# Six-layer block with a state-space scan: the four sums over states of a group are tied to the last of their four operands

## The chip, the cores and the metric

One core of one Trainium2 chip runs the whole program. The metric is the time of one execution in microseconds on the device (us), lower is better; the time before is the median of three runs.

## The reference

The input is x of shape 4 x 512 x 128 (batch, position, feature). Six residual layers follow one another: a fast-feedforward "tree" attention, a 16-head attention, the tree attention again, a mixture of 8 experts and one shared expert, a Mamba block, and the mixture again. The change lies in the Mamba block. Cut to what matters:

```
x_dbl = x @ W_x;  dt = softplus(x_dbl[..., :64] @ W_dt + b_dt)
Bm = x_dbl[..., 64:80];  Cm = x_dbl[..., 80:96];  A = -exp(A_log)      # 256 channels, 16 states
def step(h, inp):                                                      # over 512 positions
    dA = exp(dt_t[..., None] * A)
    h  = dA * h + (dt_t * x_t)[..., None] * B_t[:, None, :]
    y  = einsum('bdn,bn->bd', h, C_t)                                  # sum over the 16 states
    return h, y
y = ys + x * D;  y = y * silu(z);  out = y @ W_out;  return residual + out
```

## The kernel before

**Tiling of the scan.** `state_main` handles one batch entry b. The 256 channels are two halves c; each half is four blocks g of 32 channels; the 16 states are four groups q of four states. One tile `states` has 128 partitions, which are 32 channels times four states, and 512 positions. So a batch entry needs 2 x 4 x 4 = 32 such tiles, the four of them 128. Each goes through four steps: ScalarE takes the exponential into `decay` (L970), VectorE multiplies B with dt*x into `states` (L971) and runs the recurrence over it in place (L972), GpSimd multiplies by C in place (L973). Here "the product" is L973.

**The sums.** For one (c, q), here a "group", the function `sums` gives TensorE four matmuls (L934). Each takes one of the four `states` tiles of the group as moving operand and the constant `gather` of 128 x 32 as weights, and writes 32 partitions of the bank `state_acc`: g = 0 to 3 write partitions 0-31, 32-63, 64-95 and 96-127. The operands are f32, and each such matmul appears in the trace as two instructions, so that a group is eight. The four groups q of a half accumulate in the same bank, then `close` (L943) takes it on VectorE. There are 32 groups, 128 sums, 256 instructions.

**The order of the work.** The layers of the four batch entries overlap. Each layer of each entry is a job with planned start and end (`TIMES`), and the program is written by stepping the job that is due first. Inside `state_main`, `Later` delays the call of `sums` by five steps (`LAG_STATE`), so that it is written behind the first step of the group after next. Then the framework's scheduler lays out the order of each engine: in a simulated time of its own, an engine takes, of the instructions that are ready, the one that was written first. An instruction that is not ready when the engine is free is therefore passed by later ones of other jobs. The order so found is fixed in the program, and on the chip every engine goes through its own list in order and waits on semaphores. The four matmuls of a group are written next to one another, but nothing keeps them together: each becomes ready with its own product.

**Buffers.** `states` has eight buffers, two groups' worth; a buffer is free when its sum has read it. `state_b` (the spread B of a group, L958) has two banks, `state_acc` one.

**What else runs beside the scan.** The mixture layers' matmuls: three for each product of split operands (L173 to L175, tile `moe`), then `moe_acc` (L773), with ScalarE's tanh (L758) and VectorE's products (L759, L765) between them; GpSimd adds their results to x (L784).

Of the kernel before, what the change touches and what calls it, by code (L numbers as in the profile page):

```python
# [112 lines left out]
def macaron(ctx: ExitStack, tc: tile.TileContext, t: dict, stages: int = 6):  # L113
    nc = tc.nc
# [6 lines left out]
    def bank(role):  # L121
        return psum.tile([P, S], F32, tag=role, name=role, bufs=BANKS[role])
# [19 lines left out]
    def work(role, shape=(S,), dtype=F32):  # L142

        return wp.tile([P, *shape], dtype, tag=role, name=role, bufs=BUFS[role])
# [11 lines left out]
    def flat(a):  # L156
        return a if len(a.shape) == 2 else a.rearrange("p a b -> p (a b)")
# [763 lines left out]
    def spread(out, rows):  # L921

        nc.sync.dma_start(out=out, in_=rows.unsqueeze(1).to_broadcast([CH, OF_GROUP, S]))

    def state_main(b, st, consts):
        A = consts()[0]
        xs, sz, cs = st.xs, st.sz, st.cs
        accs = {}

        def sums(c, q, hs):  # L930
            if q == 0:
                accs[c] = bank("state_acc")
            for g in range(4):
                nc.tensor.matmul(  # L934
                    accs[c][32 * g : 32 * g + 32, :],
                    lhsT=gather,
                    rhs=hs[g],
                    start=(q == 0),
                    stop=(q == GROUPS - 1),
                )  # L940

        def close(c):
            nc.vector.scalar_tensor_tensor(  # L943
                xs[:, c, :], xs[:, c, :], at["D"][:, c : c + 1], accs[c], ALU.mult, ALU.add
            )
            nc.gpsimd.tensor_mul(xs[:, c, :], xs[:, c, :], sz[:, c, :])

        later = Later(LAG_STATE)
        for c in range(2):
            dt, dtx = work("dts", (4, S)), work("dtxs", (4, S))  # L950
            rows = t["state_rows"][b, c].rearrange("m (g r) s -> m g r s", r=CH)
            for g in range(4):
                for m, to in enumerate((dt, dtx)):
                    spread(to[:, g, :], rows[m, g])
            for q in range(GROUPS):

                bs = bank("state_b")
                nc.tensor.matmul(  # L958
                    bs,
                    lhsT=spread_b[:, ts(q, P)],  # L960
                    rhs=st.xb,
                    start=True,
                    stop=True,
                )
                hs = []
                for g in range(4):
                    k = (4 * c + g) * GROUPS + q
                    dA, h = bank("decay"), work("states")
                    hs.append(h)
                    nc.scalar.activation(dA, dt[:, g, :], AF.Exp, scale=A[:, k : k + 1])  # L970
                    nc.vector.tensor_mul(h, bs, dtx[:, g, :])  # L971
                    nc.vector.tensor_tensor_scan(h, dA, h, 0.0, ALU.mult, ALU.add)  # L972
                    nc.gpsimd.tensor_mul(h, h, cs[:, q])  # L973
                    later.step()
                    yield
                later.add(partial(sums, c, q, hs))
                if q == GROUPS - 1:
                    later.add(partial(close, c))
        while later.queue:
            later.step()  # L980
            yield
        ps = bank("state_tr")
        for i in range(NT):
            for c in range(2):
                nc.tensor.matmul(
                    ps[:, ts(i, P)],
                    lhsT=xs[:, c, ts(i, P)],
                    rhs=w_out[:, c, :],
                    start=(c == 0),
                    stop=(c == 1),  # L990
                )
        nc.vector.tensor_add(flat(x[b]), flat(x[b]), ps)
# [12 lines left out]
    def once(f):  # L1005
        made = []

        def get():
            if not made:
                made.append(f())  # L1010
            return made[0]

        return get
# [5 lines left out]
    heads, states = once(head_consts), once(state_consts)  # L1019
# [46 lines left out]
    def add_state(name):  # L1066
        b, (p0, p1, m0, m1) = int(name[1]), TIMES[name]
        st = State()
        p = job(p0, p1, 13, state_prep(b, st, states), *needs(done[b]))
        done[b] = job(m0, m1, 33 + LAG_STATE, state_main(b, st, states), p)  # L1070
# [261 lines left out]
```

## Time and profile before

| | |
|---|---|
| median of 3 runs (lowest to highest) | 1149.53 us (1147.91 to 1149.95) |
| the profiled execution, its own time | 1150.85 us |
| its span, first to last instruction | 1149.1 us |
| TensorE busy | 1080.6 us (94%) |
| VectorE busy | 909.7 us (79%) |
| ScalarE, GpSimd busy | 517.1 us (45%), 411.6 us (36%) |

The names are PE for TensorE, PEld for its weight loads, DVE for VectorE, ACT for ScalarE, POOL for GpSimd. A busy PE includes the modelled ends of pipelined matmuls, which overlap the next ones, so the distance from one start to the next tells more than a duration. In rows of the timeline the columns are start, duration, engine, line, operation, output and inputs, shapes, count, and in brackets the idle time before and what ended it.

### The profile page before, as it was taken

To read this page: it belongs to the slowest core of one execution; us is meant where nothing else is said; L and a number is where in the kernel's file an instruction comes from. 1 tells how busy PE (TensorE), PEld (TensorE's weight loads), DVE (VectorE), ACT (ScalarE), POOL (GpSimd) and SP (SyncE) were. 2 spreads that over 40 slices of the span, in tenths; PEclk is the share of its full clock that TensorE was granted. 3 is DMA by queue.
4 is the path that set the end of the run, shared out by engine and by line. 5 is a ranking of instruction groups with operands and counts; after the bars stand their busy time and mean duration, and the time that the engine had idled before them with its cause. 6 is when DMAs were issued, how large, how long until landed. Compare 5 with 4: busy or idle time off the path is not lost.

```text
span 1149.1 us, 16519 instructions
## 1 busy us (share of the span) xinstructions
PE 1080.6 (94%) x5536; PEld 715.5 (62%) x5536; DVE 909.7 (79%) x2199; ACT 517.1 (45%) x1078; POOL 411.6 (36%) x396
## 2 busy tenths in 40 slices
PE   3999999999999999999999999998798989998998
PEld 2666566566665667765566676675276656655677
DVE  5566787577676677776789998799989999999864
ACT  2221423233332455544533643565476567454444
POOL 4115322002100141320314651266626656656623
PEclk9999999999999999999999999999899999999999
DMA  7787755231442122333752334662038323823310
GB/s 208 203 248 215 260 137 122 75 94 57 85 139 60 54 58 60 104 85 112 232 181 90 125 84 122 234 210 92 1 98 278 127 60 125 292 74 124 111 51 10
DMA packets 79653, 146.42 MB, mean 127 GB/s; under 512 B 7537, under 2 KB 39665, under 8 KB 79569
## 3 DMA queue, kind: packets, MB, share of 16 engines
q1 hardware_dynamic: 79280, 145.07, 42.1%
q8 instruction: 44, 0.72, 0.3%
q14 instruction: 41, 0.33, 0.1%
q10 hardware_dynamic: 288, 0.30, 0.1%
HBM read 125.35 MB, written 13.70 MB: 121 GB/s over the span
## 4 chain that ended last, share of the span: by engine, by line
PE 63%; DVE 20%; issue 6%; DMA 4%; POOL 3%; ACT 3%; SPq 1%; POOLq 0%; ACTq 0%; DVEq 0%
PE tree_acc L404 11%; PE moe_acc L773 7%; DVE states L972 6%; PE head_acc L601 5%; PE tree_mm L173 4%; PE head_max L557 4%; PE head_sc L633 3%; PE moe L173 3%; PE tree_mm L175 3%; PE tree_mm L174 3%; DVE states L971 3%; PE moe L174 3%; PE moe L175 3%; DVE u L759 2%; PE state_acc L934 2%
## 5 line engine op out<-in xcount | busy, mean ns | idle before, releaser
L973 POOL TENSOR_TENSOR states<-states,cs 128x512 f32<-128x512 f32 x128 | 163.4, 1282 | 161.9 <-DVE states L972 93.1
L404 PE MATMUL tree_acc<-full,ring 128*128 128x512 f32 x384 | 194.3, 598 | 5.2 <-DVE full L394 4.9
L565 DVE CUSTOM_DVE_ANT_0 head_max<-head_max,kept 128x128 f32<-128x128 f32 (+3 forms) x256 | 126.8, 496 | 64.1 <-PE head_max L557 61.9
L394 DVE SCALAR_TENSOR_TENSOR full<-tree_mm,kept,mask 128x512 f32<-128x512 f32 x188 | 138.5, 746 | 40.2 <-PE tree_mm L175 35.1
L649 ACT ACTIVATE pt<-head_sc 128x512 f32<-128x512 f32 (+1 forms) x176 | 95.0, 559 | 139.0 <-PE head_sc L641 138.3
L972 DVE TENSOR_TENSOR_SCAN states<-decay,states 128x512 f32<-128x512 f32 x128 | 154.6, 1216 | 0.5
L773 PEld LDWEIGHTS moe_acc<-ring,u 128*128 128x128 f32 x1152 | 141.4, 193 | 17.6 <-DVE u L765 3.0
L773 PE MATMUL moe_acc<-ring,u 128*128 128x128 f32 x1152 | 145.7, 278 | 1.0 <-DVE u L759 0.7
L173 PE MATMUL moe<-xl,ring 128*128 128x512 f32 x288 | 128.8, 448 | 8.9 <-DVE u L765 1.9
L784 POOL TENSOR_TENSOR kept<-kept,y 128x512 f32<-128x512 f32 x64 | 83.4, 1303 | 136.2 <-ACT y L783 118.8
L970 ACT ACTIVATE decay<-dts,kept 128x512 f32<-128x512 f32 x128 | 88.4, 693 | 88.1 <-DVE states L972 66.5
L758 ACT ACTIVATE u<-moe 128x512 f32<-128x512 f32 x144 | 86.3, 602 | 70.4 <-PE moe L175 66.5
L759 DVE SCALAR_TENSOR_TENSOR u<-u,moe 128x512 f32<-128x512 f32 x144 | 97.0, 677 | 23.4 <-ACT u L758 23.1
L174 PE MATMUL moe<-xh,ring 128*128 128x512 f32 x288 | 115.4, 401 | 0.0
L175 PE MATMUL moe<-xh,ring 128*128 128x512 f32 x288 | 115.0, 400 | 0.0
L541 POOL TENSOR_SCALAR km<-k_bias,kept 128x512 fp32r<-128x512 f32 x64 | 43.3, 697 | 171.3 <-PE head_sc L633 151.0
L783 ACT ACTIVATE y<-moe_acc,scratch 128x128 f32<-128x128 f32 x256 | 73.3, 370 | 65.6 <-PE moe_acc L773 64.8
L173 PE MATMUL tree_mm<-xl,ring 128*128 128x512 f32 x188 | 96.1, 514 | 0.4 <-DVE full L394 0.2
L404 PEld LDWEIGHTS tree_acc<-full,ring 128*128 128x128 f32 x384 | 71.0, 190 | 35.8 <-issue 17.3
L173 PEld LDWEIGHTS moe<-xl,ring 128*128 128x128 f32 x288 | 54.8, 190 | 60.4 <-DVE u L765 10.4
L557 PE MATMUL head_max<-km,q_bias 120*128 120x512 f32 (+2 forms) x192 | 91.7, 479 | 0.5 <-POOL km L541 0.4
L971 DVE TENSOR_TENSOR states<-state_b,dtxs 128x512 f32<-128x512 f32 x128 | 85.6, 682 | 5.5 <-PE state_acc L934 2.6
(242 smaller groups left out, 1982.3 us busy)
## 6 DMA issues: line engine op xcount, KB each, us to landing
ring<-moe_parts SPq DMA_DIRECT2D x72, 512.0 KB
ring<-tree_parts SPq DMA_DIRECT2D x42, 512.0 KB
ring<-in_fff_w SPq DMA_DIRECT2D x24, 512.0 KB
mask<-fff_taken SPq DMA_DIRECT2D x48, 256.0 KB
ring<-in_moe_w SPq DMA_DIRECT2D x16, 512.0 KB
dts<-state_rows SPq DMA_DIRECT2D x32, 256.0 KB
dtxs<-state_rows SPq DMA_DIRECT2D x32, 256.0 KB
moe_parts<-moe_w SPq DMA_DIRECT2D x9, 512.0 KB
```

What stands on the lines that cost most here:

```text
L173: nc.tensor.matmul(ps, lhsT=lh, rhs=rl, start=start, stop=False)
L174: nc.tensor.matmul(ps, lhsT=ll, rhs=rh, start=False, stop=False)
L175: nc.tensor.matmul(ps, lhsT=lh, rhs=rh, start=False, stop=stop)
L394: nc.vector.scalar_tensor_tensor(full, ps, neg_b1[:, n : n + 1], st.masks[k][:, c, :], ALU.max, ALU.mult)
L404: nc.tensor.matmul(acc, lhsT=weights[k][1][:, c, :], rhs=h, start=(c == 0), stop=False)
L557: nc.tensor.matmul(view, lhsT=qs[:R_MAX, g, ts(i, P)], rhs=km[j0 // 2][:R_MAX, j0 % 2 : j0 % 2 + each, :kw], start=True, stop=True,)
L565: nc.vector.tensor_tensor_reduce(view[:, n, :], view[:, n, :], future[:, S - kw :], -1.0, float(np.finfo(np.float32).max), ALU.add, ALU.mi ...
L759: nc.vector.scalar_tensor_tensor(u, u, 1.0, ps1, ALU.add, ALU.mult)
L773: nc.tensor.matmul(acc[:, ts(i, P)], lhsT=h[c][:, ts(i, P)], rhs=w2[:, e % 4 * 2 + c, :], start=(c == 0), stop=(c == 1),)
L971: nc.vector.tensor_mul(h, bs, dtx[:, g, :])
L972: nc.vector.tensor_tensor_scan(h, dA, h, 0.0, ALU.mult, ALU.add)
L973: nc.gpsimd.tensor_mul(h, h, cs[:, q])
```

## The change

`sums` gets a further argument, the last of the group's four products on GpSimd (g = 3). The matmuls g = 0, 1 and 2 are given a dependency on that product, with a semaphore, beside the one on their own product. The matmul g = 3 depended on it already. Nothing is computed in another way.

```diff
-        def sums(c, q, hs):
+        def sums(c, q, hs, last):
             if q == 0:
                 accs[c] = bank("state_acc")
             for g in range(4):
-                nc.tensor.matmul(
+                mm = nc.tensor.matmul(
                     accs[c][32 * g : 32 * g + 32, :],
                     lhsT=gather,
                     rhs=hs[g],
                     start=(q == 0),
                     stop=(q == GROUPS - 1),
                 )
+                if g < 3:
+                    tc.add_manual_dep(
+                        getattr(mm, "ins", mm),
+                        last.name,
+                        mybir.DependencyInfo(
+                            mybir.DependencyClass.Sync, mybir.DependencyReason.SCHED_ONLY
+                        ),
+                        reason="sums over states begin together",
+                    )
...
-                    nc.gpsimd.tensor_mul(h, h, cs[:, q])
+                    last = nc.gpsimd.tensor_mul(h, h, cs[:, q])
                     later.step()
                     yield
-                later.add(partial(sums, c, q, hs))
+                later.add(partial(sums, c, q, hs, getattr(last, "ins", last)))
```

## The prediction

> **What bounds the kernel now.** I read the page first, then the stretches of time, then TensorE's own timeline, then the waits.
>
> The page puts the chain that ended last mostly on TensorE, with VectorE second, and the sums (L934) carry 2% of the span by themselves.
>
> ```profile
> PE 63%; DVE 20%; issue 6%; DMA 4%; POOL 3%; ACT 3%; SPq 1%; POOLq 0%; ACTq 0%; DVEq 0%
> ```
>
> That is an average over unlike stages. The scans lie between 600 and 1090 us, so I cut that stretch up: first all engines, then L934 alone. Columns: window, its length, busy us of PE, PEld, DVE, ACT, POOL (instructions), granted clock, DMA.
>
> ```profile
> 600.00:695.00 95.00, 93.56 (x492) 64.12 (x491) 93.34 (x189) 42.60 (x91) 48.70 (x41) 1.00 0.37 108
> 765.00:800.00 35.00, 32.65 (x207) 23.62 (x206) 34.48 (x64) 19.01 (x43) 20.61 (x18) 1.00 0.34 106
> 800.00:835.00 35.00, 25.64 (x74) 8.28 (x75) 32.64 (x78) 14.01 (x25) 24.25 (x22) 0.81 0.04 11
> 895.00:1000.00 105.00, 95.70 (x495) 62.83 (x493) 102.15 (x167) 67.35 (x141) 66.54 (x53) 0.98 0.43 140
> 1000.00:1090.00 90.00, 81.22 (x416) 52.62 (x417) 81.76 (x138) 43.66 (x96) 54.93 (x44) 0.98 0.34 111
> ```
> ```profile
> 600.00:695.00 95.00, 9.56 (x64) 1.42 (x64) 1.00 0.37 108
> 765.00:800.00 35.00, 5.30 (x32) 0.76 (x32) 1.00 0.34 106
> 800.00:835.00 35.00, 17.25 (x32) 2.35 (x32) 0.81 0.04 11
> 895.00:1000.00 105.00, 15.59 (x64) 2.25 (x64) 0.98 0.43 140
> 1000.00:1090.00 90.00, 18.97 (x64) 2.81 (x64) 0.98 0.34 111
> ```
>
> The reader is to see two things. While scans run, DVE is the fuller engine (93.34 of 95, 102.15 of 105); PE is a close second. And the same eight groups (64 instructions) cost PE 9.56 us in the first window and 18.97 us in the last. The timeline of PE says why.
>
> ```profile
> 910.68 1.06 PE L934 MATMUL state_acc<-states,c_state_w 128*32 128x512 f32 x8
> 911.68 2.05 PE L773 MATMUL moe_acc<-ring,u 128*128 128x128 f32 x16
> 913.96 1.05 PE L934 MATMUL state_acc<-states,c_state_w 128*32 128x512 f32 x2 [0.23 <-POOL states L973]
> 914.93 0.50 PE L173 MATMUL moe<-xl,ring 128*128 128x512 f32 x1
> ...
> 916.75 1.04 PE L934 MATMUL state_acc<-states,c_state_w 128*32 128x512 f32 x2
> 917.73 0.50 PE L173 MATMUL moe<-xl,ring 128*128 128x512 f32 x1
> ...
> 919.47 1.04 PE L934 MATMUL state_acc<-states,c_state_w 128*32 128x512 f32 x2 [0.78 <-POOL states L973]
> ```
>
> A whole group issued together (x8) holds PE from 910.68 to the next start at 911.68, 1.00 us. One sum alone (x2) holds it from 913.96 to 914.93 and from 916.75 to 917.73, 0.97 to 0.98 us. The four go side by side through the array, so four cost what one costs. Sixteen of the 32 groups stand in one piece in PE's list; the other sixteen are cut, up to four pieces.
>
> **The change, part by part.** *The tie.* The first three sums become ready with the fourth, so the scheduler should put all four in one place, behind the last product. It adds no instruction: each of the three waited for a product already and waits for a later one. A cut group then costs 1.00 instead of up to 4 x 0.98 us. If every group were whole, the eight groups in 895-1000 would take 8 x 1.00 instead of 15.59 (7.6 less), those in 1000-1090 8.0 instead of 18.97 (11.0 less), and 600-695 and 765-800 would give 1.6 and 1.3. In 800-835 (17.25 for four groups) PE has little else to do and waits for products; I count nothing there.
>
> *How much of that lies on the path.* The chain of waits, taken for the two windows where it matters, gives L934 5.7% and 11.6%:
>
> ```profile
> by line: PE moe_acc L773 16.6%; DVE states L972 13.3%; issue 6.0%; PE moe L173 5.9%; PE state_acc L934 5.7%; DVE u L765 5.2%; DVE states L971 5.1%; DMA dts<-state_rows 4.7%; DVE u L759 4.7%; PE moe L175 4.6%; PE moe L174 4.6%; POOL states L
> by line: PE moe_acc L773 14.3%; DVE states L972 13.2%; PE state_acc L934 11.6%; PE moe L173 7.9%; DVE states L971 6.8%; PE moe L174 6.7%; PE moe L175 6.5%; issue 5.5%; PE state_tr L985 4.8%; DVE u L759 3.4%; DVE u L765 2.9%; POOL xs L946 2.
> ```
>
> That is 5.7% x 105 + 11.6% x 90 = 6.0 + 10.4 = 16.4 us on the chain, out of 34.6 us busy (15.59 + 18.97). The surplus is 18.6 of the 34.6, 54%, so 8.9 us on the chain. Each piece also costs a little on both sides: in the timeline a `moe` matmul behind another starts 0.23 us after it, behind a sum 0.34 us (914.93 to 915.27), and a sum behind a `moe` matmul 0.32 us. That is 0.2 us for a piece of 0.98, a fifth more: 10.7 us. This is the upper end. The lower end is zero, because DVE stands behind PE: its idle time in the two windows is 2.9 + 8.2 = 11.1 us, of which 3.2 us are waits for `state_tr` at the end of a scan, with GpSimd before it. I take half, 5.3 us, for lack of a row that is nearer to either end: in the first window DVE is nearly full (the upper end there, 3.5, exceeds its idle 2.9), in the second it is not (7.2 against 8.2).
>
> One rule speaks of this packing: the Trainium skill, "TensorE: Matmul & The Clock Gate", Part 3 (Packing small matmuls), gives 2.38x for three 32-column tiles at N = 512. By that figure three alone (2.94 us) would take 1.24 us together, four no less, and the sixteen groups of the two windows 19.8 instead of 16: by the same working 8.4 at the upper end, 4.2 us at half. Here the trace has the duration, 1.00 for four, and it decides.
>
> *The later start of g = 0, 1, 2.* On PE, what is queued behind the waiting block are `moe` matmuls (L173) and `moe_acc` (L773). Who waits for those is ACT (L758, L783) and then DVE (L759). Before, they stood behind the first cut sum; now they stand ahead of the block, so they come earlier by up to three pieces; and what stood behind the fourth sum stays behind it. PE's waits at L934 are these:
>
> ```profile
> PE state_acc L934 <- POOL states L973: 10.2, 15, 1.4
> DVE states L971 <- PE state_acc L934: 2.6, 3, 1.4
> ```
>
> About half of the first line lies in 800-835; 5.5 us (7 times) lie in 895-1090. A group that waits up to four times will wait once, for the last product; but PE arrives at it earlier by what it saved. I take these as equal: zero, within -5.5 and +5.5.
>
> *The held buffers.* The second line is DVE waiting for a `states` buffer, priced in the rivals. *The end of a half:* `close` needs the last sum; a block of four ends at most 0.03 us later than one alone (1.00 against 0.97), eight times, 0.2 us: nothing. DMAs and GpSimd's own list are not moved by the edit itself.
>
> *The sum.* The profiled execution took 1150.85 (span 1149.1 and 1.75 around it), 1.3 above the median; 1150.85 - 5.3 = 1145.5 there, and 1149.53 - 5.3 = 1144.2 against the median, which I forecast. 0.2% is 2.3 us here, about what a measurement of this kernel can tell from no change.
>
> **The rivals.** *(a) Saved time turns into waiting: no change.* Where DVE and GpSimd set the pace, PE only reaches the block sooner and stands until the last product. For it: DVE's 102.15 of 105; the stalls of 0.23 and 0.78 in front of lone sums, which mean that PE follows GpSimd closely. Against it: 8.2 us of idle DVE in the last window, and chain pieces on L934. Time 1149.5, within 2.3.
>
> *(b) Held buffers: slower.* The first three `states` buffers of a cut group stay taken until the fourth product is done, and VectorE, which runs ahead into the group after next, finds none. The place is L971. The price of one such wait shows here:
>
> ```profile
> 1076.58 0.69 DVE L971 TENSOR_TENSOR states<-state_b,dtxs 128x512 f32<-128x512 f32 x1 [1.35 <-PE state_acc L934]
> ```
>
> The lone sum before it started at 1075.50. Of the cut groups, 14 lie outside 800-835; one such wait in each is 14 x 1.35 = 18.9 us, less the 5.3 saved: 13.6 slower. One in half of them: 9.5 - 5.3 = 4.2 slower, 1153.7. It decides from the fourth wait on (5.3 / 1.35 = 3.9), and is slower by over 0.2% from the sixth. For it: VectorE is the fullest engine, waits of this kind exist already, and this one is for a sum just finished, not one long done. The order that the scheduler finds changes behind each block, and can make more of them. Against it: only 2.6 us in all today, and in most cut groups the product two groups on starts over 4 us after the whole group's sums are done.
>
> *(c) The tie does not join them.* The scheduler could still put other work between the four. Ready at the same moment and written side by side, they should stay together; this would end within (a).
>
> **How the numbers follow.** Forecast (faster): 0.47, its own range 1138.8 (all 10.7) to 1147.2. No change, (a) and (c): 0.13. Slower, (b): 0.40, since DVE is the fuller engine through most of the scans and a list reordered in 16 places has many chances to make it wait. The range takes the upper end of the gain and (b) up to about ten waits (13.5 - 5.3 = 8.2, to 1157.7): 1139 to 1158, leaving out some 2 in 10.
>
> **What would show it.** Right: L934 stands as x8 nearly everywhere, its busy time in the two windows falls from 34.6 to about 16 to 20 us, and DVE's wait at L971 for L934 stays near 2.6 us. (a): the same, with PE's waits at L934 grown by about what was saved. (b): DVE's wait at L971 for L934 at 8 us or more. Wrong altogether: L934 still cut, or the difference in a stretch before 660 us, where every group is whole already.

## The result, and the profile after

| | before | after |
|---|---|---|
| median of 6 runs (lowest to highest), same chip | 1149.03 us (1147.91 to 1149.95) | 1157.36 us (1154.73 to 1160.41) |
| ratio, 95% interval | | 1.0075 [1.0056, 1.0094] |
| the profiled execution, its time and span | 1150.85, 1149.1 us | 1160.41, 1158.5 us |

Slower by 8.3 us. The tie's code is added below the sums, so their line is still L934; the lines behind it move: the exponential is now L980, B times dt*x into `states` L981, the recurrence L982, the product L983, the spread `state_b` L968, `state_tr` L995.

The chain by engine first. TensorE's share has grown from 63% to 65%.

```profile
PE 65%; DVE 19%; issue 6%; DMA 3%; POOL 3%; ACT 3%; SPq 0%; POOLq 0%; ACTq 0%; DVEq 0%
```

Next the stretches. The work is now later by up to 10 us, so the windows are shifted to hold the same groups: first all engines in the lone stretch and the last one, then L934 alone in all five.

```profile
805.00:840.00 35.00, 19.63 (x76) 8.85 (x77) 32.55 (x78) 14.81 (x26) 24.31 (x22) 0.61 0.05 14
1006.00:1100.00 94.00, 81.29 (x414) 53.78 (x414) 82.66 (x137) 44.02 (x96) 55.29 (x44) 0.91 0.32 108
```
```profile
600.00:691.50 91.50, 10.47 (x64) 1.55 (x64) 1.00 0.35 100
770.00:805.00 35.00, 5.30 (x32) 0.76 (x32) 1.00 0.35 106
805.00:840.00 35.00, 6.87 (x32) 0.76 (x32) 0.61 0.05 14
900.00:1006.00 106.00, 12.68 (x64) 1.81 (x64) 1.00 0.42 137
1006.00:1100.00 94.00, 15.46 (x64) 2.06 (x64) 0.91 0.32 108
```

The groups of the last two windows cost 28.1 us instead of 34.6: of the surplus of 18.6 us that the prediction wanted to remove, 6.4 us went. Part of the 15.46 us is a lower clock: it was 0.91 in that window, against 0.98 before. PE's own timeline shows what became of a tied group, and two lines of the waits what stands around it.

```profile
1020.49 1.92 PE L934 MATMUL state_acc<-states,c_state_w 128*32 128x512 f32 x2
1022.34 2.77 PE L773 MATMUL moe_acc<-ring,u 128*128 128x128 f32 x16
1025.04 1.06 PE L934 MATMUL state_acc<-states,c_state_w 128*32 128x512 f32 x6
```
```profile
PE state_acc L934 <- POOL states L983: 13.7, 5, 4.5
DVE states L981 <- PE state_acc L934: 3.7, 3, 2.4
```

One sum goes alone (x2), sixteen `moe_acc` matmuls come next, and the other three follow (x6). In PE's list L934 stood in 47 pieces before and stands in 43 now; 21 groups of 32 are in one piece, against 16. (Neighbouring groups that touch count as one piece here; counted group by group it is 55 pieces before, 44 after, and 32 would be all whole.) VectorE's wait for held buffers went from 2.6 to 3.7 us only.

Where is the time lost? The end of each group's fourth product is a mark that both kernels have. The table (worked out from the traces, not a view of the profile) gives how many us later than in the profiled run of before it comes; groups 0 to 7 are batch entry 0, 8 to 15 entry 1, and so on; "end" is the last matmul. That run of before itself loses some 1.3 us between groups 23 and 25 and again at its end, so all rows fall there; steps within a row count, not levels. Each row is one execution: where two kernels have the same lists, steps of about 1 us still occur (0.6 to 1.7 between groups 0 and 7 in the row of entry 2).

```
group                          0    7    8   15   19   20   24   25   26   28   31  end
after                        0.2  0.1  6.6  4.8  4.9  6.7  6.7  7.5 10.8 10.7  8.9  9.4
tie in entry 0              -0.1 -0.2  4.6  3.5  4.0  4.0  2.7  2.0  2.0  2.0  2.0  0.6
the same, SyncE in order     0.4  0.3  2.0  1.1  1.1  1.2  0.6 -0.1 -0.1 -0.1 -0.1 -1.9
whole, SyncE in order        0.0 -0.1  1.6 -0.1 -0.6  1.4 -0.1 -0.7  2.4  2.1  0.3  0.8
whole, in order, not g. 19   0.3  0.3  1.9  0.1  1.5  1.6  0.8  0.3  1.8  2.6  0.6  1.0
tie in entry 2               0.6  1.7  2.1  2.1  2.7  4.5  3.4  2.7  2.7  2.7  2.7  1.3
tie in first half, entry 3  -0.9 -0.9 -0.9 -0.9 -0.2 -0.2 -1.0 -1.7  1.7  1.5  1.3 -0.1
```

After loses its time in three steps: 6.5 us between groups 7 and 8, 1.8 between 19 and 20, some 3 around 26. The first lies where hardly a sum is running. SyncE's queue shows it; first before, then after (columns: start, duration, queue, line, operation, count).

```profile
680.90 0.32 SPq L357 DMA_DIRECT2D fff_taken<-taken  x1
682.74 0.32 SPq L154 DMA_DIRECT2D ring<-tree_parts  x1
683.48 2.76 SPq L363 DMA_DIRECT2D mask<-fff_taken  x4
687.21 0.33 SPq L154 DMA_DIRECT2D ring<-tree_parts  x1
```
```profile
682.58 0.32 SPq L357 DMA_DIRECT2D fff_taken<-taken  x1
683.25 2.10 SPq L154 DMA_DIRECT2D ring<-tree_parts  x2
685.47 2.61 SPq L363 DMA_DIRECT2D mask<-fff_taken  x4
```
```profile
DVE full L394 <- DMA mask<-fff_taken: 3.6, 1, 3.6
PE tree_mm L173 <- DVE full L394: 3.9, 1, 3.9
```

Before, the four mask loads of a tree layer (L363) left between the two 512 KB ring loads (L154); after, both ring loads leave first. The masks are asked for 2 us later and stand behind 512 KB more. VectorE waits 3.6 us for them at L394 and PE 3.9 us for VectorE. In the profile of before the first of these waits is 0.4 us; in other traces with the old order of the loads it is up to 1.1 us (1.1 with the tie in the second half of entry 3 alone). No instruction of that layer, the second tree layer of batch entry 3, is in the diff: the tie moved sums of entry 0 in the scheduler's simulated time, and the order it then found for SyncE is another one.

### The profile page after: what moved, and what is told of

Same layout as the page of the kernel before. It is cut to its first block, busy times and chain, and to the rows that moved or that the text cites. A ratio compares the mean times of both kernels' runs of the same rounds, so it can differ in the third digit from the quotient of the medians.

```text
span 1158.5 us, 16518 instructions
## 1 busy us (share of the span) xinstructions
PE 1074.8 (93%) x5536; PEld 717.2 (62%) x5536; DVE 909.0 (78%) x2199; ACT 516.8 (45%) x1078; POOL 411.0 (35%) x396
## 4 chain that ended last, share of the span: by engine, by line
PE 65%; DVE 19%; issue 6%; DMA 3%; POOL 3%; ACT 3%; SPq 0%; POOLq 0%; ACTq 0%; DVEq 0%
PE tree_acc L404 11%; PE moe_acc L773 7%; DVE states L982 6%; PE head_acc L601 4%; PE tree_mm L173 4%; PE moe L173 4%; PE head_max L557 4%; PE head_sc L633 3%; PE moe L174 3%; PE moe L175 3%; PE tree_mm L175 3%; DVE states L981 3%; PE tree_mm L174 3%; DVE u L759 2%; DVE u L765 2%
## 5 line engine op out<-in xcount | busy, mean ns | idle before, releaser
L983 POOL TENSOR_TENSOR states<-states,cs 128x512 f32<-128x512 f32 x128 | 163.3, 1281 | 160.6 <-DVE states L982 98.2
L394 DVE SCALAR_TENSOR_TENSOR full<-tree_mm,kept,mask 128x512 f32<-128x512 f32 x188 | 138.4, 745 | 45.3 <-PE tree_mm L175 37.9
L982 DVE TENSOR_TENSOR_SCAN states<-decay,states 128x512 f32<-128x512 f32 x128 | 153.9, 1211 | 0.5
L773 PEld LDWEIGHTS moe_acc<-ring,u 128*128 128x128 f32 x1152 | 141.8, 194 | 19.8 <-DVE states L982 3.2
L773 PE MATMUL moe_acc<-ring,u 128*128 128x128 f32 x1152 | 146.3, 279 | 1.8 <-DVE u L759 1.1
L173 PE MATMUL moe<-xl,ring 128*128 128x512 f32 x288 | 129.4, 451 | 14.4 <-DVE states L981 4.4
L980 ACT ACTIVATE decay<-dts,kept 128x512 f32<-128x512 f32 x128 | 88.6, 695 | 89.5 <-DVE states L982 67.9
L173 PE MATMUL tree_mm<-xl,ring 128*128 128x512 f32 x188 | 96.6, 516 | 4.3 <-DVE full L394 4.1
L173 PEld LDWEIGHTS moe<-xl,ring 128*128 128x128 f32 x288 | 54.9, 191 | 65.3 <-DVE states L982 11.3
L404 PEld LDWEIGHTS tree_acc<-full,ring 128*128 128x128 f32 x384 | 71.5, 191 | 34.6 <-issue 17.8
L981 DVE TENSOR_TENSOR states<-state_b,dtxs 128x512 f32<-128x512 f32 x128 | 85.0, 677 | 7.3 <-PE state_acc L934 3.7
```

Of the source, the lines that this page charges most:

```text
L173: nc.tensor.matmul(ps, lhsT=lh, rhs=rl, start=start, stop=False)
L394: nc.vector.scalar_tensor_tensor(full, ps, neg_b1[:, n : n + 1], st.masks[k][:, c, :], ALU.max, ALU.mult)
L404: nc.tensor.matmul(acc, lhsT=weights[k][1][:, c, :], rhs=h, start=(c == 0), stop=False)
L773: nc.tensor.matmul(acc[:, ts(i, P)], lhsT=h[c][:, ts(i, P)], rhs=w2[:, e % 4 * 2 + c, :], start=(c == 0), stop=(c == 1),)
L983: last = nc.gpsimd.tensor_mul(h, h, cs[:, q])
```

## The experiments

Three theories go through the expectations. **A:** the order of the lists, SyncE's above all. **B:** buffers held longer (the prediction's rival (b)). **C:** the waits that the change adds on PE. Ratios are to the kernel before, run beside on the same chip; brackets are 95% intervals.

**1. One batch entry at a time.** Four kernels with the tie for one entry each:

```diff
-                if g < 3:
+                if g < 3 and b == 0:      # then 1, 2, 3
```

Entry 0: 

> The tie for batch entry 0 alone (groups 0 to 7), nothing tied in the other three. Theory A (order of the queues: a 512 KB ring load has moved ahead of the mask loads of a tree layer on SP, and VectorE stood 3.6 us for a mask at 691.5): this part alone brings most of the loss, +5 to +6.5 us against before, and the wait of VectorE at L394 for the mask loads is there, 3 to 4 us. Theory B (held buffers of states, the slower rival of the prediction): VectorE had no wait for L934 in this entry, so 0 within 1 us. Theory C (TensorE's queue stands at the block for the last product): no such wait in this entry either, 0 within 1 us.

Entry 1: 

> The tie for batch entry 1 alone (groups 8 to 15, with the stretch in which little else runs). In the changed kernel the lag behind before shrank here from 6.6 to 4.8 us, at the fourth products of the groups. Theory A, by these progress points: -1 to -2 us. Theory B: 0 to +2 (no VectorE wait for L934 was seen here). Theory C: TensorE stands 4.3, 2.3 and 4.5 us at the blocks in this entry and its clock is halved from 805 to 833 us, so +1 to +4.

Entry 2: 

> The tie for batch entry 2 alone (groups 16 to 23); the lists of VectorE and SP are those of before, TensorE's alone differs. In the changed kernel the lag grew by 1.8 us between the products of groups 19 and 20, where VectorE waited 2.1 us for a convolution of the next entry's scan. Theory A: +1 to +2.5. Theory B: 0 within 1, no wait of VectorE for L934 was seen in this entry.

Entry 3: 

> The tie for batch entry 3 alone (groups 24 to 31). In the changed kernel the lag grew here from 6.7 to 10.6 us and ended at 9.4. Theory A: +2 to +3, from a changed place of the sums on TensorE and no change on SP worth naming. Theory B: all of VectorE's waits for L934 lie here (2.4 + 0.3 + 1.1 us in the changed kernel, against 2.6 before), so +1 to +3 from this, and most of the whole loss if B is the main cause (+5 to +8). Theory C: 0 to +2.

Measured: entry 0 1.0029 [1.0014, 1.0045], entry 1 0.9991 [0.9975, 1.0006], entry 2 1.0014 [1.0004, 1.0024], entry 3 1.0015 [1.0001, 1.0029]. The sum, +0.49%, lies in one interval of the whole (0.37 to 0.78, experiment 2) and just below the other (0.56 to 0.94). Entry 0 cost less than theory A had it, 3.3 us against 5 to 6.5, and its wait for the masks was 1.8 us against 3 to 4. The step between groups 7 and 8 belongs to entry 0 alone; the step between 19 and 20 to entry 2 (table). Each kernel's lists differ from those of before in the stretch of its own entry and are the same again after it.

**2. SyncE's order put back.** The tie stays; the second ring load of that one layer is told to stand behind the fourth mask load in SyncE's list, with no semaphore. It was run with the tie in entry 0 and with the whole change. Cut to what matters:

```diff
-            move(w[m], t["tree_parts"][:, k, m, :])
+            ring = move(w[m], t["tree_parts"][:, k, m, :])
+            if m and mask is not None:   # that one layer only
+                behind(ring, mask)       # add_manual_dep, NoSync, SCHED_ONLY
```

Entry 0: 

> As the kernel with the tie for batch entry 0 alone, and one further ordering without a semaphore: the second part of that tree layer's third ring load is issued behind the four mask loads, as before the change. The tie and TensorE's new places for the sums stay. Theory A: the wait for the mask falls from 3.6 to under 1 us, and the time goes back to within 1.5 us of before (1149.0). Theories B and C: the order of SP's loads is not the cause, the time stays where the tie for entry 0 alone put it.

The whole change again, as it is: 

> The whole change once more, as the measure for the three beside it on the same chip. All theories: slower than before by 0.56 to 0.94% (the interval of the first comparison).

The whole change, SyncE in order: 

> The whole change, with the one further ordering on SP: the second part of the tree layer's third ring load behind the four mask loads. Theory A: as for the tie of entry 0, where it took 3.4 us back, this is 3 to 5 us faster than the whole change, and what is left over before is 2 to 5 us, from entries 2 and 3. Theory B (held buffers): within 1 us of the whole change.

Measured: entry 0 0.9999 [0.9984, 1.0014] instead of 1.0029; the whole 1.0058 [1.0037, 1.0078] as it is, 1.0034 [1.0022, 1.0046] in order. Putting SyncE's order back is worth 0.24 to 0.30%, about 3 us; for entry 0 the two intervals only touch, for the whole they overlap. It is not the one load alone: the scheduler lays out everything behind it anew. With the tie in entry 0 SyncE's whole list is again that of before, and PE's list differs from that without the swap in 15 places, VectorE's in 22, all between 690 and 725 us. Up to 690 us the tied sums stay where the tie put them. SyncE's timeline of the entry 0 kernel, in order (thirteen lines more stand above, so L357, L363 and L394 are L369, L375 and L407), and the row of `full` in the answer for the tile `mask` (duration min, median, max in ns, then first and last start):

```profile
682.78 0.32 SPq L369 DMA_DIRECT2D fff_taken<-taken  x1
...
684.55 2.61 SPq L375 DMA_DIRECT2D mask<-fff_taken  x4
```
```profile
L407 DVE SCALAR_TENSOR_TENSOR full<-tree_mm,kept,mask x9: 719/743/754, 690.4 to 704.0; 128x512 f32<-128x512 f32 x9
```

The mask loads leave only 0.9 us earlier than in after (684.55 against 685.47), but VectorE's first `full` starts at 690.4; in after at 695.1, before at 690.1. (In the kernel with the tie in entry 0, without the swap, the loads leave at 685.18 and `full` starts at 693.09.) The wait for the masks is gone. What stays of the step at group 8, 6.5 us in after, is 1.7 us: `taken` itself is still late (682.78; before, 680.90). From 669 us on the lists of PE and VectorE are other ones, with the sums of groups 6 and 7 moved; that this makes `taken` late is argued.

**3. The order without the waits.** The tie orders the scheduler's lists but sets no semaphore.

```diff
-                            mybir.DependencyClass.Sync, mybir.DependencyReason.SCHED_ONLY
+                            mybir.DependencyClass.NoSync, mybir.DependencyReason.SCHED_ONLY
```

> The change with the tie as an ordering for the scheduler alone, without a semaphore: on the chip each sum waits only for its own product. The lists of all engines are those of the changed kernel up to some 830 us and differ a little behind. Theory A (the order): the lag of 4 to 6 us at the products of group 8 (755.1 us before) stays, and the whole stays slower, by 4 to 9 us. Theory C (the added waits): lag at group 8 under 1 us, the whole within 2 us of before.

Measured: 1.0040 [1.0025, 1.0055], with the step at group 8 (0.5 to 6.4 us) and the mask wait (3.0 us) as in after. Without any added wait most of the loss is there: theory C falls for the first step. (Behind some 830 us these lists are no longer those of after, so the difference to 1.0058 tells nothing of the waits.)

**4. One group of entry 2.** The lists of the entry 2 kernel differ from those of before on PE, in eleven places, most of them at group 19, and on ScalarE, where three instructions of group 19's stretch and one at 985 us change places; VectorE's, GpSimd's and SyncE's are the same.

```diff
-                if g < 3:
+                if g < 3 and (b, c, q) == (2, 0, 3):
```

> Only one group is tied, the last group of the first half of batch entry 2 (sums at 914 to 925 us before). Theory A: its three deferred sums stand in front of the next entry's projection matmul, VectorE's wait for conv goes from 0.3 to about 2 us, the lag at the group after is 1.8 us, and the whole is 1.0010 to 1.0016, the whole cost of tying entry 2. Theory B (held buffers): this group holds three buffers longer, VectorE waits at L971 for L934, no step between groups 19 and 20. If neither: 0.9995 to 1.0005.

Measured: 1.0019 [1.0009, 1.0029]. It is a little over theory A's upper end. VectorE's waits in 905-960, before and then here, and PE's timeline here:

```profile
DVE conv L853 <- ACT conv L849: 0.3, 1, 0.3
```
```profile
DVE conv L853 <- ACT conv L849: 2.1, 1, 2.1
```
```profile
914.77 0.50 PE L173 MATMUL moe<-xl,ring 128*128 128x512 f32 x1 [0.86 <-DVE states L982]
...
917.52 0.49 PE L173 MATMUL moe<-xl,ring 128*128 128x512 f32 x1 [0.81 <-ACT v L762]
...
924.48 1.04 PE L934 MATMUL state_acc<-states,c_state_w 128*32 128x512 f32 x2
...
926.46 1.05 PE L934 MATMUL state_acc<-states,c_state_w 128*32 128x512 f32 x4
927.44 0.33 PE L318 MATMUL moe_tr<-kept,ln 128*128 128x128 f32 x1
927.70 1.04 PE L934 MATMUL state_acc<-states,c_state_w 128*32 128x512 f32 x2
928.68 0.50 PE L173 MATMUL state<-xl,w_in 128*128 128x512 f32 x1
```

Before, the four sums of this group stood at 913.96, 916.75, 919.47 and 924.26, the first and the third behind stalls of 0.23 and 0.78 us. Without the first three PE stands in this stretch all the same, 0.86 and 0.81 us in the rows shown, for VectorE and ScalarE, and it comes to its next sum at 924.48 instead of 924.26: to take them out has gained nothing. Tied, they come together as three pieces in front of the projection of the next entry (tile `state`, L173), which starts at 928.68 instead of 926.72. ScalarE's and then VectorE's `conv` wait for it, 1.8 us longer, and the lag grows by those 1.8 us (0.3 to 2.1 between groups 19 and 20). Theory A, on PE's own list this time: the sums that were early and cheap are now late and in the way.

**5. The whole change, SyncE in order, without group 19.** This is the kernel of experiment 2 with `(b, c, q) != (2, 0, 3)` added.

> The whole change, with the ring load behind the mask loads again, and without the tie of group 19. Theory A (order of the queues): the two causes add up, and what is left is entry 3: 1.0034 less 0.0014 to 0.0019, so 1.0010 to 1.0020; no step of lag between groups 19 and 20, a step of 1 to 2 us between groups 25 and 26. Theory C (added waits): 1.003 or more.

Measured: 1.0022 [1.0012, 1.0032], 0.12% less than with group 19 tied (the intervals overlap), and no step between 19 and 20; but its row has a step of 1.4 us between groups 15 and 19, most of it at group 17, where this trace has half clock from 879.7 us and sixteen `moe_acc` matmuls last 3.68 us instead of 2.05. The ratio is a little over the forecast's upper end, its interval reaches well into the forecast; the step around group 26 is what stays.

**6. Entry 3 taken apart.** The tie for its first half (c == 0), its second half (c == 1), and for its second group alone.

First half: 

> Only the four groups of the first half of batch entry 3 are tied. Theory B (held buffers, which is the wait of 2.4 us at L981 seen there): the whole cost of entry 3 lies here, 1.0010 to 1.0020, with VectorE's wait for L934 at 3 us or more. Otherwise 0.9995 to 1.0005.

Second half: 

> Only the four groups of the second half of batch entry 3 are tied, the last of the kernel. Theory B: 0.9990 to 1.0005, the cost lies in the first half. If the end of the kernel is what pays (the last group's sums and what follows them): 1.0010 to 1.0020.

Group 25: 

> Only one group is tied, the second of batch entry 3. Three places in PE's list change, none in VectorE's or SyncE's. Theory B (held buffers): VectorE waits about 2.4 us at L971 for the late sums, and the time grows by as much or more, 1.0015 to 1.0025. Theory A: the wait shows, but the mixture matmuls that went ahead give most of it back; 0.9995 to 1.0010.

Measured: first half 1.0016 [1.0006, 1.0027], second half 1.0002 [0.9991, 1.0014], group 25 alone 1.0014 [1.0003, 1.0025]. By these the first half carries all of entry 3. DVE's timeline with the first half tied:

```profile
1016.96 0.69 DVE L981 TENSOR_TENSOR states<-state_b,dtxs 128x512 f32<-128x512 f32 x1 [2.35 <-PE state_acc L934]
```

VectorE stands 2.35 us for a held buffer, theory B's place, because three of the four sums of group 25 were put behind sixteen `moe_acc` matmuls, as in the rows of after above. Its waits for L934 in the stretch are 3.7 us; before, 1.3. In number this is what theory B had.

But the order is only part of it. The whole change was traced twice, with the same lists on every engine. The first trace is that of after, the second that of the run beside experiment 2. First all engines in the seven us around group 25 (the granted clock is the third number from the end), then the rows of the second trace, and the wait of VectorE in both.

```profile
1017.00:1024.00 7.00, 6.41 (x16) 3.50 (x17) 6.69 (x16) 2.59 (x4) 3.79 (x3) 0.51 0.01 2
```
```profile
1016.00:1023.00 7.00, 6.26 (x33) 3.39 (x33) 6.33 (x15) 3.13 (x7) 3.17 (x4) 1.00 0.00 0
```
```profile
1018.43 1.05 PE L934 MATMUL state_acc<-states,c_state_w 128*32 128x512 f32 x2 [0.39 <-POOL states L983]
1019.41 2.05 PE L773 MATMUL moe_acc<-ring,u 128*128 128x128 f32 x16
1021.39 1.06 PE L934 MATMUL state_acc<-states,c_state_w 128*32 128x512 f32 x6
```
```profile
1026.19 0.69 DVE L981 TENSOR_TENSOR states<-state_b,dtxs 128x512 f32<-128x512 f32 x1 [2.38 <-PE state_acc L934]
```
```profile
1022.54 0.69 DVE L981 TENSOR_TENSOR states<-state_b,dtxs 128x512 f32<-128x512 f32 x1 [0.58 <-PE state_acc L934]
```

At half clock the lone sum and the sixteen `moe_acc` hold PE for 4.55 us (1020.49 to 1025.04 in after), at full clock for 2.96 us, and VectorE's wait is 2.38 or 0.58 us. This holds for all seven traces with group 25 tied by semaphore (those with priority aside): 2.15 to 2.38 us in the four with half clock at this place (after, entry 3, its first half, and the whole with SyncE in order), 0.57 to 0.58 us in the three with full clock (the second trace of the whole, the one without group 19, and group 25 alone). The step of lag between groups 25 and 26 goes with it: 3.1 to 3.4 us in the four, 0.8 to 1.5 us in the three (three of these traces are not in the table). So the order by itself costs about 1 us in these traces, and half clock, where it falls here, some 2 us more. How often it falls here in the twelve runs of a kernel is not known: each has one trace. The runs' mean clock points the same way: 0.986 with the first half tied, 0.988 with group 25, 0.989 with the second half, 0.990 before.

Group 25 alone missed both theories: the wait of 2.4 us did not come, and its ratio lies above theory A's range. Its step of 0.8 us lies within its interval (0.3 to 2.9 us).

**7. Groups that are truly whole.** Since the tie left most cut groups cut, the sums were given priority in the scheduler as well, with and without SyncE put in order.

```diff
             for g in range(4):
-                mm = nc.tensor.matmul(
+              with tc.high_priority():
+                mm = nc.tensor.matmul(
```

> All groups tied, and the four sums of a group also have priority in the scheduler, so that nothing ready gets between them. Does joining itself pay? If the term of the prediction was right and only the joining failed: L934 busy in 895-1090 falls from 34.6 to about 16 to 18 us, and the time falls by 5.3 us against the whole change; the mask loads still stand behind the ring load here, so by theory A (order of the queues) some 3.3 us of loss stay: about 1151, ratio 1.000 to 1.003. Theory C (joined sums only move the wait, GpSimd and VectorE set the pace): L934 falls as much, PE's waits at L934 grow, and the time stays near that of the whole change, 1.005 to 1.008.

> As the run with priority, and the second ring load of the tree layer is put behind the four mask loads again. Theory A: about 0.3% below the run with priority, no wait of VectorE for the masks above 1 us; if joining pays as the prediction's sum had it (5.3 us), 1144 to 1146, ratio 0.995 to 0.998. If joining is worth nothing (theory C), 1149 to 1154, ratio 1.000 to 1.004.

Measured: 1.0199 [1.0181, 1.0217] and 1.0182 [1.0160, 1.0203]. Both expectations missed by more than 1%. L934 did fall nearly as far as expected (19.3 us for the last sixteen groups, in 895 to 1110, against 16 to 18), and putting SyncE in order took off 0.17%, with overlapping intervals. Since priority alone might be the cause, it was run on the kernel before, without the tie:

> No tie at all; the four sums of a group only have priority in the scheduler, so that each goes as soon as its own product is done (104 pieces instead of 47). If being whole is what costs 2% in the run with tie and priority (one block waits for the last product and holds what stands behind it on TensorE): here PE's waits at L934 stay near the 10 us of before, and the time is 0.998 to 1.008. If priority itself costs it (sums in front of all other work): 1.015 or more, with waits at L934 as in that run (42 us).

Measured: 1.0733 [1.0714, 1.0753]. The group of L934 in the four kernels (busy us, mean ns, idle time before them and what ended it): before, after, tie and priority, priority alone. With one more line above, L934 becomes L935 in the last two.

```profile
L934 PE MATMUL state_acc<-states,c_state_w 128*32 128x512 f32 x256 | 66.7, 632 | 15.8 <-POOL states L973 10.2 <-DVE states L972 4.2 <-DVE u L765 0.9
```
```profile
L934 PE MATMUL state_acc<-states,c_state_w 128*32 128x512 f32 x256 | 50.9, 654 | 16.2 <-POOL states L983 13.7 <-DVE scratch L271 1.9 <-DVE states L981 0.2
```
```profile
L935 PE MATMUL state_acc<-states,c_state_w 128*32 128x512 f32 x256 | 39.0, 684 | 42.6 <-POOL states L984 42.4 <-DVE xs L954 0.2
```
```profile
L935 PE MATMUL state_acc<-states,c_state_w 128*32 128x512 f32 x256 | 126.2, 619 | 45.5 <-POOL states L974 45.0 <-DVE xs L944 0.2
```

| | pieces | L934 busy | PE's wait there for the product | ratio |
|---|---|---|---|---|
| before | 47 | 66.7 us | 10.2 us | 1 |
| after | 43 | 50.9 | 13.7 | 1.0058 and 1.0075 |
| tie and priority | 31 | 39.0 | 42.4 | 1.0199 |
| priority alone | 104 | 126.2 | 45.0 | 1.0733 |

Three things follow. Joining seems to pay where sums have priority: between the last two rows the waits are alike (42.4, 45.0), L934 is 87.2 us shorter, and the time 61.9 us (1234.19 to 1172.29), 0.7 us for each us; but the lists of all engines differ between the two, so this is no price of joining alone. Priority is what costs: against before it adds 34.8 us of PE's waits and 59.5 us of L934 alone, 94.3 together, and the time grows by 84.8. And wholeness bought with priority loses: 27.7 us less of L934, 32.2 us more of PE's waits at the block, and behind the block VectorE waits for `state_b` (1.5 to 10.2 us), `conv` (1.2 to 5.5) and `xs` (0.5 to 4.3). The gaps between the pieces of a cut group were filled with other jobs' matmuls; a block at the front of the list stands until the last product is there. The Trainium skill, "TensorE: Matmul & The Clock Gate", Part 3 (The mechanism), says that matmuls start and end strictly in program order, and the 42.4 us agree: nothing behind the block went past it.

## Why the prediction was wrong, point by point

- **"The scheduler should put all four in one place", and rival (c) dismissed with "they should stay together": this step failed first.** 47 pieces became 43, not 31, and 11 of the 16 cut groups stayed cut. It is what the prediction itself named as a sign of "wrong altogether: L934 still cut". Being ready together is not being taken together: by the scheduler's rule it takes what was written first, and after the first sum older `moe_acc`, `moe` and `moe_tr` matmuls went ahead of the other three (x2, L773 x16, x6). The term of 18.6 us surplus measured 6.4 (some of the rest is the lower clock). By the prediction's own working (47% of it on the chain, a fifth more for each piece) that is worth 3.6 us at most, 1.8 at half; no run shows a gain of that size by itself, the nearest being entry 1 with 0.9991, whose interval holds 1.
- **"DMAs and GpSimd's own list are not moved by the edit itself": this failed for the most money.** No DMA is in the diff, but SyncE's list is laid out by the same scheduler in the same simulated time, and it changed: 3.6 us of waiting for masks in the profile of after, 1.8 to 3.0 in the other traces with that order and no priority, and 0.24 to 0.30%, a third to a half of the loss (experiment 2). The prediction asked who waits behind each moved matmul on PE, and never what the new order does to the other queues.
- **The later start of g = 0, 1, 2, "zero, within -5.5 and +5.5":** group 19 alone costs 1.8 us in the lag, 0.12 to 0.19% in the three comparisons that hold it. PE's waits for the product in the last two windows did go down, from 5.5 us (7 times) to 2.5 (2 times); the cost came up behind the block. The prediction quoted its stalls of 0.23 and 0.78 us as a sign that PE follows GpSimd closely, and did not see that the lone sums there were free, since PE stands there without them too: to take them out saves nothing, and to put them later costs their full time.
- **Rival (b), held buffers:** right in kind and place (L971, now L981), wrong in number: one long wait, not seven, and 3.7 us in all against 2.6. The size of that wait, 2.4 us against its 1.35, is mostly the clock: at full clock it is 0.58 us (experiment 6). Its 1153.7 lay nearer to the result than the forecast, but by a sum that was not what happened. For the same reason it is luck that 1157.36 lies just inside the range of 1139 to 1158: the upper end stood for ten such waits.
- **Rival (a), nothing changes because time turns to waiting:** PE's wait at L934 grew from 10.2 to 13.7 us, but 11.2 of it lie in the lone stretch, where they cost nothing; in the last two windows it fell (above). It describes the kernel with tie and priority better than the change.
- **The first stretch:** 600-695 was to give 1.6 us of L934; it rose there from 9.56 to 10.47.
- **Right:** 1.00 us for a whole group; the lone stretch as no part of the sum: L934 fell there from 17.25 to 6.87 us and the time did not move.
- **The account.** SyncE's order 0.24 to 0.30%, group 19 0.12 to 0.19%, the first half of entry 3 (order, held buffer and clock together) 0.16%: 0.52 to 0.65%, against 0.58% [0.37, 0.78] and 0.75% [0.56, 0.94] for the whole. By these values at most some 0.2% stays unexplained; each part has an interval of 0.10 to 0.24% to either side, so the sum agrees with the whole and does not prove that nothing else took part. How the 0.16% divides between order and clock stays open. What made the scheduler choose each of the new orders was argued from its rule, not traced.

## What to carry to other kernels

A dependency that looks local can re-lay the lists of all engines and of the DMA queue: before costing what it does on its own engine, compare every queue's order before and after, and look for loads that a full engine waits for. Before a wait is put down to an order, look at the granted clock there, and at a second trace of the same program. Where PE's list is packed by a scheduler, small matmuls that sit in gaps of the producer can be free, as they were at group 19; to gather them saves their time only if the gaps go too, and it may put them in front of something that was on time. A change that touches many places is priced place by place: tied entry by entry and group by group, the loss came apart into a few waits of 2 to 4 us.

## What the runs showed of the hardware

- In the lone stretch of entry 1 PE's granted clock fell further when the four sums came as one block with idle time before them: 0.61 in 805-840 after, 0.81 in 800-835 before, and a block of eight there has the duration 1.94 us instead of 1.06. The Trainium skill, "TensorE: Matmul & The Clock Gate", Part 1 (HAM oscillation), puts the limit at idle gaps of about 3.4 us. The gaps in front of the three slow blocks are 4.34, 2.34 and 4.52 us, but half clock begins at 805.4 us, 0.5 us into the first of them. Group 25 agrees still less. With the first half of entry 3 tied, half clock begins there at 1007.8, and the longest gap in the ten us before is 1.96 us; and the two traces of the whole change have alike gaps in front of group 25 (1.90 and 0.69 or 0.70 us), one at half clock and one at full. A single gap of 3.4 us is not the limit here; what is, no run shows.
- The half clock of the lone stretch cost nothing that could be measured: with the tie in entry 1 alone the clock there is just as low (0.66 in 800-840, as in the run without group 19), and the time is 0.9991 [0.9975, 1.0006]. PE waits there for GpSimd (11.2 us in after). At group 25 half clock fell where VectorE waits for PE, and its wait was 2.2 to 2.4 us instead of 0.6. So what half clock costs depends on the place where it falls.
- Four sums of 512 f32 columns side by side in the array took 1.00 us from start to start, one alone 0.98, at full clock.
- From the first of the four mask loads to the first `full` it was 7.9 to 9.7 us in the four traces (without priority) in which both 512 KB ring loads left ahead of them, and VectorE waited for the masks in all four; it was 5.8 to 7.4 us in the eleven in which one did. In the matched pair (tie in entry 0, without and with the swap) the masks were issued 0.6 us later (685.18, 684.55) and `full` started 2.7 us later (693.09, 690.39). So the time of the issue alone does not tell when a load counts; that the bytes in flight ahead of it make the rest is argued, not shown.
